# Gathering the last edge slots of a group's first block for 32 or 64 nodes instead of 128

## The chip, the cores and the metric

The kernel runs on one core of a Trainium2 chip. The metric is the device time of one launch in microseconds (us); the number given for a kernel is the median of several runs.

A core has a matrix engine (PE, with its weight load PEld), a vector engine (DVE), a scalar engine (ACT), a general engine (POOL) and a queue engine (SP). On-chip memory has 128 partitions, so a tile holds up to 128 nodes, one per partition. Plain transfers are issued from SP. Transfers whose rows are picked by a list of indices (gathers and scatters, "indirect DMAs") are issued from POOL.

## The reference

One layer of a graph network over 6,250 nodes with 256 features and 206,250 directed edges (100,000 random pairs in both directions, and a loop for each node). What matters here is the attention over edges:

```python
xn = _layernorm(x, axis=-1)
q, k, v = xn @ Wq.T + bq, xn @ Wk.T + bk, xn @ Wv.T + bv      # 8 heads of 32
sim = (q[dst] * k[src]).sum(head) / sqrt(32)                   # one number per edge and head
attn = softmax of sim over the edges with the same dst
agg[n] = sum over edges with dst == n of attn * v[src]
x = x + agg @ Wo.T + bo + linear_attention(xn)
x = x + mixture_of_experts(_layernorm(x))                      # 8 experts, each node goes to one
```

The edges come sorted by `dst`, so each node's sources lie next to each other, and a node's degree is the number of its edges: 33 on average.

## The kernel before

**Tables.** A first stage (about 138 us) computes keys and values of all nodes, block by block of 128, and writes them to a table in device memory, `kv_tab`, with 512 floats (2 KB) per node.

**Groups and blocks.** The 49 blocks of nodes form three groups of 20, 17 and 12 blocks (`GROUPS`). In each group the nodes are sorted by falling degree (`rank_group`), and the sorted nodes are cut into blocks of 128 again. So the first block of a group (block 0, 20 and 37) holds the nodes with the most edges, the highest degree in partition 0. A block has a fixed number of slots (`SLOTS`, from `planned_slots`); slot `j` holds the `j`-th edge of each of its 128 nodes. A first block has 62 slots, since it has to hold the node of the highest degree; the second blocks have 43, 43 and 41. All blocks together have 1,715 slots. A node with fewer edges than slots has rows of other edges in the rest; they are masked by a large negative number (`late`, L1358).

**Units and chunks.** A block's slots are cut into units of at most 44 slots (a first block has two units of 31), and a unit into chunks of four or five (`W = 5`). A chunk is one buffer `kvg` of a ring of 11 (`kvp`, `RING`). For each slot one indirect DMA on POOL (L627) brings the 128 rows of `kv_tab` that the slot's indices name, 256 KB. In the main loop (from L1355 on) the DVE multiplies the keys of a chunk by the queries (L1373) and adds them up per head (L1374). After a unit's last chunk comes the softmax, and the values of this unit are weighted on the DVE (L1325) and added by the PE (matmul with the identity, L1329, into `pa`) while the keys of the next unit are worked on. Only then is the buffer free again. POOL's instructions stand in one order: `gather_to(at + 1 + LEAD)` lets the gathers run ahead of the keys by `LEAD = 2` chunks in that order, and in time POOL goes as far ahead as free buffers of the ring let it.

**Work beside.** `background` puts pieces of other work between the chunks, paced by the number of slots: in group 0's attention the queries, the sorting of the other groups (`other_ranks`) and the linear attention; in group 1's and 2's attention the output projection, routing and experts of the group before (`behind`). This work starts with the second unit of a group's first block at the latest. After the last group's attention its own experts follow with nothing beside them.

**Guard.** `other_ranks` compares each node's degree with its block's slots (L687, `over`). If any node has more, a flag is set and a general path runs after the fast one.

Of the kernel before, what the change touches and what calls it, by code (L numbers as in the profile page):

```python
# [42 lines left out]
def planned_slots(n_nodes, n_edges, groups):  # L43

    lam = max(1.0, n_edges / n_nodes - 1.0)
    pm = [math.exp(-lam)]
    for k in range(1, 1000):  # L50
        pm.append(pm[-1] * lam / k)
    more = [sum(pm[k:]) for k in range(len(pm))]
    out, b0 = [], 0
    for g in groups:
        m = min(n_nodes - b0 * P, g * P)
        for j in range(g):
            k = 1
# [5 lines left out]
            out.append(k)  # L63
        b0 += g
    return out

# [2 lines left out]
def gps_layer(  # L69
# [50 lines left out]
    C = max(1, math.ceil(1.25 * N / NX))  # L120
    MI = MH * MD
    HP = MI // P
    SLOTS = planned_slots(N, E, GROUPS)
    SMAX = max(SLOTS)
    scale = 1.0 / math.sqrt(GD)

# [31 lines left out]
    with tc.manual_schedule():  # L158
# [207 lines left out]
        with ExitStack() as actx:  # L366
# [210 lines left out]
            for b in order:  # L577
                S = SLOTS[b]
                n_p = -(-S // PART)
                cut = [S * i // n_p for i in range(n_p + 1)]  # L580
                for i in range(n_p):
                    n = cut[i + 1] - cut[i]
                    n_ch = -(-n // W)
                    cuts = [cut[i] + n * k // n_ch for k in range(n_ch + 1)]
                    units.append((b, i, n_p, cut[i], cut[i + 1], list(zip(cuts, cuts[1:]))))
            chunk_list = [(u, k) for u in range(len(units)) for k in range(len(units[u][5]))]
            UMAX = max(u[4] - u[3] for u in units)
            idx_of, qs_of, kv_of = {}, {}, {}
# [24 lines left out]
            def gather_to(k):  # L613

                nonlocal pool_at
                while pool_at < min(k, len(chunk_list)):
                    u, c = chunk_list[pool_at]
                    b, part, _, _, _, chunks = units[u]
                    i = order.index(b)
                    if c == 0 and part == 0 and i > 0:  # L620
                        sources(i + 1)
                        queries(i + 1)
                    j0, j1 = chunks[c]
                    kv = kvp.tile([P, W, 2 * D], F32, name="kvg")
                    kv_of[u, c] = kv
                    for j in range(j0, j1):
                        nc.gpsimd.indirect_dma_start(  # L627
                            out=kv[:, j - j0, :], out_offset=None, in_=kv_tab[:, :],
                            in_offset=bass.IndirectOffsetOnAxis(ap=idx_of[b][:, j : j + 1], axis=0),
                        )  # L630
                    pool_at += 1

# [48 lines left out]
        def other_ranks():  # L681
            t = rank_consts(mp1)
            for g in range(1, NG):
                yield from rank_group(g, t, mp1, mp2)
            bs = list(range(NB))
            for b in bs:
                nc.vector.tensor_scalar(over[:, b : b + 1], deg_r[:, b : b + 1], float(SLOTS[b]), None, op0=ALU.is_gt)  # L687
                if b % 8 == 7:
                    yield 1.5
            nc.vector.tensor_reduce(bad[:, 1:2], over, AX.X, ALU.max)  # L690
# [624 lines left out]

        def weigh(v, c):

            j0, j1 = v["chunks"][c]
            m = j1 - j0
            kv = kv_of.pop((v["u"], c))  # L1320
            if c == 0:
                v["pa"] = qps.tile([P, D], F32, name="pa")
            s0, s1 = v["s0"], v["s1"]
            vals = kv[:, :m, D:].rearrange("p j (h d) -> p j h d", d=GD)
            nc.vector.tensor_tensor(  # L1325
                vals, vals, v["pr"][:, j0 - s0 : j1 - s0, :, None].to_broadcast([P, m, GH, GD]), ALU.mult
            )
            for j in range(m):
                nc.tensor.matmul(  # L1329
                    v["pa"], ident, kv[:, j, D:], start=(j0 + j == s0), stop=(j0 + j == s1 - 1),  # L1330
                )

        def complete(v):
# [21 lines left out]
        for u, (b, part, n_p, s0, s1, chunks) in enumerate(units):  # L1355
# [4 lines left out]
            )  # L1360
            sim = cp2.tile([P, UMAX, GH], F32, name="sim")[:, :n, :]
            n_v = len(v["chunks"]) if v else 0
            for c in range(max(len(chunks), n_v)):
                work = pace[group_of[b]] * (chunks[c][1] - chunks[c][0] if c < len(chunks) else W)
                background(work / 2)
# [2 lines left out]
                background(work / 2)  # L1368
                if c < len(chunks):
                    gather_to(at + 1 + LEAD)  # L1370
                    j0, j1 = chunks[c]
                    keys = kv_of[u, c][:, : j1 - j0, :D]
                    nc.vector.tensor_tensor(keys, keys, qc[:, None, :].to_broadcast([P, j1 - j0, D]), ALU.mult)  # L1373
# [588 lines left out]
```

## Time and profile before

| | us |
|---|---|
| median of 3 runs | 3531.13 (3529.72 to 3541.31) |
| profiled execution | 3071.36 |
| its span, first to last instruction | 3069.6 |

The profiled execution is 460 us shorter than the median of the runs. The profile doesn't show why.

Busy time of each engine in stretches of the profiled execution (us from the start of its span):

| stretch | what runs | length | PE | DVE | POOL |
|---|---|---|---|---|---|
| 0 to 138 | keys, values, first sort | 138 | 118.36 | 88.29 | 52.38 |
| 138 to 480 | group 0's attention, its first blocks | 342 | 196.98 | 251.35 | 224.15 |
| 480 to 1200 | rest of group 0, start of group 1 | 720 | 535.27 | 598.97 | 547.03 |
| 1200 to 1365 | group 1, its first blocks | 165 | 119.04 | 145.64 | 104.55 |
| 1365 to 2100 | rest of group 1, start of group 2 | 735 | 540.54 | 476.65 | 550.58 |
| 2100 to 2250 | group 2, its first blocks | 150 | 99.22 | 119.00 | 77.20 |
| 2250 to 2740 | rest of group 2 | 490 | 393.37 | 290.35 | 340.49 |
| 2740 to 3069 | last group's experts and output | 329 | 214.93 | 56.47 | 27.46 |

An engine that is busy for a large part of a stretch need not be its limit; the waits say which one is. A POOL instruction for an indirect DMA counts as busy only while it runs, and each is followed by a gap of 0.30 us, so that a POOL with nothing to wait for shows about three quarters.

### The profile page before, as it was taken

What the parts mean: (1) busy time and instruction counts of PE and PEld (TensorE: products, weight loads), DVE (VectorE), ACT (ScalarE), POOL (GpSimd) and SP (SyncE); (2) the same over time, 40 slices, a digit from 0 to 9 for tenths busy, and PEclk for the clock granted to TensorE, in tenths of its full rate; (3) what the DMA queues carried; (4) which work ended last, traced back from release to release, by engine and by line L of the source; (5) the groups of instructions that cost most, each with busy time, mean ns of one, the idle gap of its engine ahead of it and who ended that gap; (6) DMA issues with size and microseconds to landing.
All of it is one profiled execution on the core that took longest, in us unless ns stands there. A gap on an engine that the chain in (4) does not pass through costs nothing. (4 is left out here: it accounts for less than half of the span.)

```text
span 3069.6 us, 29584 instructions
## 1 busy us (share of the span) xinstructions
PE 2217.7 (72%) x9090; PEld 1731.0 (56%) x9090; DVE 2026.7 (66%) x2728; ACT 638.1 (21%) x1800; POOL 1923.8 (63%) x2114
## 2 busy tenths in 40 slices
PE   8756548788788655764989988445629999856494
PEld 4335335555555444643777877334528888735494
DVE  5658868898888767884767766566845666664000
ACT  4300003343434101210111111101202122112242
POOL 4366767777777777567777777776466767650101
PEclk9867779999898778876999999678859999978797
DMA  7675876777777668767888887777668988753783
GB/s 256 212 248 171 268 260 201 213 211 213 208 206 221 199 197 262 250 195 234 307 285 307 294 301 248 223 204 248 198 188 279 321 300 311 241 179 111 279 327 111
DMA packets 294378, 728.05 MB, mean 237 GB/s; under 512 B 47142, under 2 KB 156292, under 8 KB 280900
## 3 DMA queue, kind: packets, MB, share of 16 engines
q0 software_dynamic: 149744, 477.83, 50.7%
q1 hardware_dynamic: 144468, 248.24, 23.2%
q8 instruction: 75, 1.23, 0.2%
q14 instruction: 91, 0.75, 0.1%
HBM read 652.25 MB, written 73.64 MB: 236 GB/s over the span
## 5 line engine op out<-in xcount | busy, mean ns | idle before, releaser
L627 POOL DMA_INDIRECT kvg<-kv_tab,idx x1715 | 1628.3, 949 | 650.7 <-issue 463.2
L1329 PE MATMUL pa<-kvg,ident 128*128 128x256 f32 x3430 | 1008.4, 451 | 583.3 <-DVE kvg L1325 420.6
L1329 PEld LDWEIGHTS pa<-kvg,ident 128*128 128x128 f32 x3430 | 756.9, 227 | 817.1 <-DVE kvg L1325 501.4
L1373 DVE TENSOR_TENSOR kvg<-kvg,qc 128x1280 f32<-128x1280 f32 (+1 forms) x366 | 512.4, 1400 | 389.3 <-DMA kvg<-kv_tab,idx 326.7
L1374 DVE TENSOR_REDUCE sim<-kvg 128x40 f32<-128x1280 f32 (+1 forms) x366 | 513.2, 1402 | 12.6
L1325 DVE TENSOR_TENSOR kvg<-kvg,pr 128x1280 f32<-128x1280 f32 (+1 forms) x366 | 509.3, 1393 | 0.0
L1204 PE MATMUL bank<-wt,hTe 128*128 128x256 f32 x1056 | 247.7, 382 | 0.0
L1187 PE MATMUL bank<-xTe,wt 128*128 128x256 f32 x1056 | 242.6, 381 | 2.3 <-ACT xTe L1177 2.3
L1187 PEld LDWEIGHTS bank<-xTe,wt 128*128 128x128 f32 x1056 | 201.6, 191 | 30.5 <-ACT xTe L1177 3.0
L1204 PEld LDWEIGHTS bank<-wt,hTe 128*128 128x128 f32 x1056 | 201.7, 193 | 27.5
L1268 DVE TENSOR_TENSOR res<-bank,row_b 128x256 f32<-128x256 f32 x49 | 20.6, 421 | 280.8 <-ACT bank L1264 272.6
L751 PE MATMUL bank<-wm,xTm 128*128 128x512 f32 x392 | 178.0, 597 | 0.0
L1247 POOL DMA_INDIRECT row_a<-ybuf,row_from x49 | 46.5, 948 | 197.6 <-DMA ybuf<-res 173.0
L1193 ACT ACTIVATE hTe<-bank,wt 128x256 f32<-128x256 f32 x264 | 110.8, 471 | 266.0 <-PE bank L1187 266.0
L1210 ACT COPY res<-bank 128x256 f32<-128x256 f32 x85 | 31.7, 372 | 424.5 <-PE bank L1208 236.1
L751 PEld LDWEIGHTS bank<-wm,xTm 128*128 128x128 f32 x392 | 72.1, 194 | 71.6 <-issue 71.3
L1301 ACT COPY qc<-qs 128x256 f32<-128x256 f32 x49 | 18.8, 384 | 442.9 <-DVE kvg L1373 412.0
L843 POOL DMA_INDIRECT xbuf<-row_a,row_to x49 | 48.0, 980 | 96.6 <-DVE cmp L1088 67.5
L537 PE MATMUL pkv<-wn,xT 128*128 128x512 f32 (+1 forms) x276 | 106.0, 540 | 3.5 <-DVE kv L552 3.5
L843 POOL DMA_INDIRECT agg_tab<-ag,node_ri x49 | 48.5, 990 | 91.2 <-DVE ag L1347 68.4
L1173 PE MATMUL bank<-ident,in 128*128 128x128 f32 x170 | 28.7, 283 | 100.4 <-DMA in<-xbuf 100.4
L780 ACT ACTIVATE ck<-bank,rk 128x64 f32<-128x64 f32 x392 | 86.2, 341 | 28.9 <-DVE rk L777 28.4
(258 smaller groups left out, 2208.4 us busy)
## 6 DMA issues: line engine op xcount, KB each, us to landing
wt<-in_w_rows_dram SPq DMA_DIRECT2D x33, 1152.0 KB, 8.2
wt<-in_w_rows_dram SPq DMA_DIRECT2D x33, 1028.0 KB, 7.9
kvg<-kv_tab,idx POOLq DMA_INDIRECT x1715, 4.0
kvg<-in_w_rows_dram SPq DMA_DIRECT2D x19, 1152.0 KB, 6.1
kvg<-in_w_rows_dram SPq DMA_DIRECT2D x19, 1028.0 KB, 7.7
kv_tab<-kv SPq DMA_DIRECT2D x49, 256.0 KB, 2.7
in<-xbuf SPq DMA_DIRECT2D x85, 128.0 KB, 8.7
ybuf<-res SPq DMA_DIRECT2D x85, 128.0 KB, 3.4
```

Source lines behind the costliest of these rows:

```text
L537: nc.tensor.matmul(done[i], xTs[b // GX][:, b % GX, c, :], wn[:, c, w], start=(c == 0), stop=(c == DC - 1))
L627: nc.gpsimd.indirect_dma_start(out=kv[:, j - j0, :], out_offset=None, in_=kv_tab[:, :], in_offset=bass.IndirectOffsetOnAxis(ap=idx_of[b][: ...
L751: nc.tensor.matmul(pm, xT_of[b][:, c, :], wmf[:, c, s * MI : (s + 1) * MI], start=(c == 0), stop=(c == DC - 1),)
L780: nc.scalar.activation(cks[b][:, h, :], pms[b][0][:, h * MD : (h + 1) * MD], AF.Copy, scale=rk[:, h : h + 1])
L843: s = nc.gpsimd.indirect_dma_start(**kw)
L1187: nc.tensor.matmul(ph[:, k, :], w[:, c, f * P : (f + 1) * P], T[t]["xT"][:, c, :size], start=(k == 0 and c == 0), stop=(k == 1 and c == DC ...
L1193: nc.scalar.activation(T[t]["hT"][:, f, :size], ph[:, k, :], AF.Relu, bias=w1_t[:, V1 + f : V1 + f + 1])
L1204: nc.tensor.matmul(py, T[t]["hT"][:, f, k * P : (k + 1) * P], w[:, f, :], start=(f == 0), stop=False)
L1325: nc.vector.tensor_tensor(vals, vals, v["pr"][:, j0 - s0 : j1 - s0, :, None].to_broadcast([P, m, GH, GD]), ALU.mult)
L1329: nc.tensor.matmul(v["pa"], ident, kv[:, j, D:], start=(j0 + j == s0), stop=(j0 + j == s1 - 1),)
L1373: nc.vector.tensor_tensor(keys, keys, qc[:, None, :].to_broadcast([P, j1 - j0, D]), ALU.mult)
L1374: nc.vector.tensor_reduce(sim[:, j0 - s0 : j1 - s0, :], keys.rearrange("p j (h d) -> p j h d", d=GD), AX.X, ALU.add)
```

## The change

`planned_slots` now returns, for each block, a list with a number of nodes for each slot. In a group's first block it works out from a Poisson distribution of degrees how many of the group's nodes are expected to use slot `s`, adds 2.5 standard deviations and 1, and takes the smallest of 32, 64 and 128 that is not below it. All slots of other blocks keep 128. For this input, block 0 and 20 get 45 slots of 128, 2 of 64 and 15 of 32; block 37 gets 44, 2 and 16. Since the nodes are sorted, the first partitions are those with the most edges.

Chunks are now cut so that all slots of one have the same number of nodes. The second units of the first blocks had seven chunks of 4, 4, 5, 4, 4, 5, 5 slots; in block 0 and 20 they have seven of 4, 5, 5 (128 nodes), 2 (64) and 5, 5, 5 (32), in block 37 eight of 4, 4, 5, 2, 4, 4, 4, 4. The number of slots, 1,715, stays. In a chunk of `n` nodes the gather, both multiplications, the reduction and the matmul use partitions 0 to `n` only. The entries of `sim` of these slots are set to 0 first (one memset of the DVE for each of the three units), so that the other partitions have a value there, which the mask makes negligible. The guard compares in a first block partitions 0 to 31, 32 to 63 and 64 to 127 with their own number of slots (62, 47 and 45; in block 37 62, 46 and 44).

```diff
+            nodes = [P] * k
+            for s in range(k if j == 0 else 0):
+                p = more[s]
+                need = m * p + 2.5 * math.sqrt(max(0.0, m * p * (1 - p))) + 1
+                nodes[s] = next(n for n in (32, 64, P) if need <= n or n == P)
+            out.append(nodes)
...
-                    n_ch = -(-n // W)
-                    cuts = [cut[i] + n * k // n_ch for k in range(n_ch + 1)]
-                    units.append((b, i, n_p, cut[i], cut[i + 1], list(zip(cuts, cuts[1:]))))
+                    chunks = []
+                    for nodes in (P, 64, 32):
+                        js = [j for j in range(cut[i], cut[i + 1]) if NODES[b][j] == nodes]
+                        n_ch = -(-len(js) // W)
+                        cuts = [js[0] + len(js) * k // n_ch for k in range(n_ch + 1)] if js else []
+                        chunks += [(j0, j1, nodes) for j0, j1 in zip(cuts, cuts[1:])]
+                    units.append((b, i, n_p, cut[i], cut[i + 1], chunks))
...
                         nc.gpsimd.indirect_dma_start(
-                            out=kv[:, j - j0, :], out_offset=None, in_=kv_tab[:, :],
-                            in_offset=bass.IndirectOffsetOnAxis(ap=idx_of[b][:, j : j + 1], axis=0),
+                            out=kv[:n, j - j0, :], out_offset=None, in_=kv_tab[:, :],
+                            in_offset=bass.IndirectOffsetOnAxis(ap=idx_of[b][:n, j : j + 1], axis=0),
                         )
...
-                nc.vector.tensor_scalar(over[:, b : b + 1], deg_r[:, b : b + 1], float(SLOTS[b]), None, op0=ALU.is_gt)
+                for p0, n in ((0, P),) if min(NODES[b]) == P else ((0, 32), (32, 32), (64, 64)):
+                    q = slice(p0, p0 + n)
+                    most = sum(m > p0 for m in NODES[b])
+                    nc.vector.tensor_scalar(
+                        over[q, b : b + 1], deg_r[q, b : b + 1], float(most), None, op0=ALU.is_gt
+                    )
...
-            vals = kv[:, :m, D:].rearrange("p j (h d) -> p j h d", d=GD)
+            vals = kv[:n, :m, D:].rearrange("p j (h d) -> p j h d", d=GD)
             nc.vector.tensor_tensor(
-                vals, vals, v["pr"][:, j0 - s0 : j1 - s0, :, None].to_broadcast([P, m, GH, GD]), ALU.mult
+                vals, vals, v["pr"][:n, j0 - s0 : j1 - s0, :, None].to_broadcast([n, m, GH, GD]), ALU.mult
             )
             for j in range(m):
                 nc.tensor.matmul(
-                    v["pa"], ident, kv[:, j, D:], start=(j0 + j == s0), stop=(j0 + j == s1 - 1),
+                    v["pa"], ident[:n, :], kv[:n, j, D:], start=(j0 + j == s0), stop=(j0 + j == s1 - 1),
                 )
...
+            few = [j0 for j0, _, m in chunks if m < P]
+            if few:
+                nc.vector.memset(sim[:, few[0] - s0 :, :], 0.0)
...
-                    keys = kv_of[u, c][:, : j1 - j0, :D]
-                    nc.vector.tensor_tensor(keys, keys, qc[:, None, :].to_broadcast([P, j1 - j0, D]), ALU.mult)
+                    keys = kv_of[u, c][:m, : j1 - j0, :D]
+                    nc.vector.tensor_tensor(
+                        keys, keys, qc[:m, None, :].to_broadcast([m, j1 - j0, D]), ALU.mult
+                    )
                     nc.vector.tensor_reduce(
-                        sim[:, j0 - s0 : j1 - s0, :], keys.rearrange("p j (h d) -> p j h d", d=GD), AX.X, ALU.add
+                        sim[:m, j0 - s0 : j1 - s0, :], keys.rearrange("p j (h d) -> p j h d", d=GD), AX.X, ALU.add
                     )
```

More of the change, by code (lines that the diff above doesn't have):

```diff
@@ L62, in planned_slots @@
                 k += 1
-            out.append(k)
+            nodes = [P] * k
[4 more added lines that the diff above has]
+            out.append(nodes)
         b0 += g
@@ L122, in gps_layer @@
     HP = MI // P
-    SLOTS = planned_slots(N, E, GROUPS)
+    NODES = planned_slots(N, E, GROUPS)
+    SLOTS = [len(n) for n in NODES]
     SMAX = max(SLOTS)
@@ L622, in gather_to @@
                         queries(i + 1)
-                    j0, j1 = chunks[c]
+                    j0, j1, n = chunks[c]
                     kv = kvp.tile([P, W, 2 * D], F32, name="kvg")
@@ L1316, in weigh @@
         def weigh(v, c):
-            j0, j1 = v["chunks"][c]
+            j0, j1, n = v["chunks"][c]
             m = j1 - j0
@@ L1370, in gps_layer @@
                     gather_to(at + 1 + LEAD)
-                    j0, j1 = chunks[c]
-                    keys = kv_of[u, c][:, : j1 - j0, :D]
-                    nc.vector.tensor_tensor(keys, keys, qc[:, None, :].to_broadcast([P, j1 - j0, D]), ALU.mult)
+                    j0, j1, m = chunks[c]
+                    keys = kv_of[u, c][:m, : j1 - j0, :D]
+                    nc.vector.tensor_tensor(
+                        keys, keys, qc[:m, None, :].to_broadcast([m, j1 - j0, D]), ALU.mult
+                    )
                     nc.vector.tensor_reduce(
-                        sim[:, j0 - s0 : j1 - s0, :], keys.rearrange("p j (h d) -> p j h d", d=GD), AX.X, ALU.add
+                        sim[:m, j0 - s0 : j1 - s0, :], keys.rearrange("p j (h d) -> p j h d", d=GD), AX.X, ALU.add
                     )
```

## The prediction

> **What bounds the kernel now.** I read the engines' shares of the span first, then the groups of instructions, then POOL's own order of time, and last who waits for whom just behind the slots that the change touches.
>
> ```profile
> PE 2217.7 (72%) x9090; PEld 1731.0 (56%) x9090; DVE 2026.7 (66%) x2728; ACT 638.1 (21%) x1800; POOL 1923.8 (63%) x2114
> L627 POOL DMA_INDIRECT kvg<-kv_tab,idx x1715 | 1628.3, 949 | 650.7 <-issue 463.2
> L1373 DVE TENSOR_TENSOR kvg<-kvg,qc 128x1280 f32<-128x1280 f32 (+1 forms) x366 | 512.4, 1400 | 389.3 <-DMA kvg<-kv_tab,idx 326.7
> ```
>
> No engine looks full, but two rows name the bound of the attention: the gathers' POOL instructions are followed by 463 us of "issue", gaps in which POOL waits for nothing visible, and the DVE waits 327 us for gathered data. POOL's order of time shows the gap:
>
> ```profile
> 600.20 0.94 POOL L627 DMA_INDIRECT kvg<-kv_tab,idx  x1 [0.30 <-issue]
> 601.45 0.95 POOL L627 DMA_INDIRECT kvg<-kv_tab,idx  x1 [0.30 <-issue]
> 602.70 0.95 POOL L627 DMA_INDIRECT kvg<-kv_tab,idx  x1 [0.30 <-PE pa L1329]
> ```
>
> A gather starts every 1.25 us: 0.95 and a fixed 0.30. From 475 to 1250 us POOL has no longer gap than that, so there each gather is worth its 1.25 us. The narrow gathers lie elsewhere. Counting L627 in POOL's order, those of block 0 (slots 45 to 61 of a block that starts at the 38th gather) run from 274 to 296 us, block 20's from 1189 to 1210, block 37's from 2088 to 2113. Just behind them (waits of POOL, then of the DVE, from 1212 to 1337 us):
>
> ```profile
> POOL kvg L627 <- PE pa L1329: 13.4, 8, 5.4
> POOL agg_tab L843 <- DVE ag L1347: 6.2, 1, 6.2
> POOL kvg L627 <- PE bank L890: 5.8, 5, 4.5
> ...
> DVE row_b L917 <- PE bank L911: 6.3, 7, 1.4
> DVE rsd L932 <- ACT rsd L926: 3.7, 4, 1.7
> DVE logits L952 <- PE bank L949: 1.4, 1, 1.4
> DVE kvg L1373 <- issue: 1.1, 1, 1.1
> ```
>
> Here POOL waits for free buffers (PE pa is the last reader of one) and for the DVE, and the DVE never waits for gathered data. The same in order of time, POOL's first such waits and the DVE's first wait for data behind each first block:
>
> ```profile
> 336.86 0.94 POOL L627 DMA_INDIRECT kvg<-kv_tab,idx  x1 [2.47 <-PE pa L1329]
> 361.69 1.49 DVE L1373 TENSOR_TENSOR kvg<-kvg,qc 128x1280 f32<-128x1280 f32 x1 [2.61 <-DMA kvg<-kv_tab,idx]
> 1251.54 0.94 POOL L627 DMA_INDIRECT kvg<-kv_tab,idx  x1 [4.54 <-PE bank L890]
> 1337.54 1.49 DVE L1373 TENSOR_TENSOR kvg<-kvg,qc 128x1280 f32<-128x1280 f32 x1 [0.72 <-DMA kvg<-kv_tab,idx]
> 2131.73 0.94 POOL L627 DMA_INDIRECT kvg<-kv_tab,idx  x1 [4.74 <-PE pa L1329]
> 2247.92 1.49 DVE L1373 TENSOR_TENSOR kvg<-kvg,qc 128x1280 f32<-128x1280 f32 x1 [4.55 <-DMA kvg<-kv_tab,idx]
> ```
>
> In all three places POOL is stopped by the full ring before the DVE next lacks data. At the start of a group the work beside is dense on the DVE (57.8 of 63 us busy from 298 to 361, 108.5 of 125 from 1212 to 1337, 106.1 of 132 from 2115 to 2247). So in the profiled execution the DVE is the limit exactly where the change makes POOL faster.
>
> **What the Trainium skill says.** *DMA: Bandwidth & Descriptors*, section "Anatomy of one DMA — SWDGE (gpsimd) path", calls descriptor generation "small, variable" and says "You can emit a lot of descriptors before the incremental cost shows up": a 32-row gather could cost POOL nearly what a 128-row one does. The trace agrees only in that bytes don't matter (0.945 us for an index load of up to 248 B a row, 0.949 for 2 KB); all indirect DMAs here have 128 rows, so it shows no price of a row. *Perfetto Trace Analysis*, section "DMA Instruction — SWDGE (GPSIMD)", says that the instruction's end in the profile is the end of descriptor generation, which fits data that land 4.0 us after the issue. *TensorE: Matmul & The Clock Gate*, section "LDWEIGHTS (loading the stationary operand)": "A 32×128 weight load takes the same time as a 128×128 weight load". *VectorE: DVE Perf Modes*, section "Why `tensor_reduce` can't reduce along partition axis", describes the partitions as independent lanes that stream along the free dimension, so fewer partitions save the DVE nothing. No run shows either with fewer partitions yet.
>
> **The change part by part.**
> - *Narrow gathers.* 46 of 32 rows and 6 of 64. POOL's saving for one lies between 0 (all of it fixed) and the share of missing rows times the whole period. With half of the period per row, the middle of these bounds since no row of the trace narrows them, a 32-row gather saves 0.5 × 0.75 × 1.25 = 0.47 us and a 64-row one 0.31. That is 7.7 us each for block 0 and 20 (15 × 0.47 + 2 × 0.31), 8.1 for block 37, 23.5 in all; at most 47. In the profiled execution all of it goes into POOL's waits for the ring: next late is what is late now, the DVE. Counted on the path: 0.
> - *Fewer bytes.* (46 × 96 + 6 × 64) × 2 KB = 9.8 MB of 728. Where they fall, the DVE doesn't wait for data. 0.
> - *DVE.* The two multiplications and the reduction of a chunk fit 0.16 us + 1.04 ns per element (1.486 us for 1,280, 1.220 for 1,024), by elements per partition, which don't change in sum. One chunk more in block 37: 3 × 0.16 = 0.5. Three memsets of 136 or 144 elements at the 0.19 of the 160-element memset of `ones`: 0.6. Six more comparisons at the 0.143 of `over`: 0.9, at 336 to 351 us. Together 2.0 us on the engine that is full there; what the DVE waits for data soon after hides some of it. 0 to 2.0, taken as 2.0.
> - *PE.* 104 of the 3,430 matmul instructions of L1329 have 32 or 64 rows of weights. Taken at no cost by the skill; what it is if the narrow loads no longer hide is rival C.
> - *Ring and order.* Block 37's second unit has eight chunks, but the second blocks of 41 and 43 slots have nine, so the ring sees nothing new. No instruction of SP, ACT or POOL is added, none moves past another; on the DVE a chunk's work shifts by a piece of work beside at most.
>
> Sum against the profiled execution: 3071.4 + 0 to 2 us.
>
> **From there to the median.** The median, 3531.1, is 459.8 us above the profiled execution, as much as 0.229 us on each of the 2,009 indirect DMAs (1,715 and 6 × 49). The profile can't say whether it lies there. But POOL is what bounds most of the attention, so an extra on another engine would have to exceed POOL's waits first. If it lies on POOL, its period is 1.477 us, and the waits that swallow the saving shrink. That gives the cases.
>
> **A, faster (0.48), the forecast: the extra lies on POOL, and half a gather's period goes by rows.** A 32-row gather then saves 0.554 us, a 64-row one 0.369: 9.05 us each in block 0 and 20, 9.6 in block 37. Slack behind block 0: 2.2 us of POOL waits above 0.30 (298 to 361 us), less 49 DMAs × 0.229 = 11.2: none, so all 9.05 stay. Behind block 20: 11.0 + 5.9 + 4.3 = 21.2 less 84 × 0.229 = 19.2 leaves 2.0, so 7.05 stay. Behind block 37 (2115 to 2247): 46.6 less 72 × 0.229 = 16.5 leaves 30, so nothing stays. 16.1 − 2.0 = 14.1, and 3531.1 − 14.1 = **3517 us**. With all of the period by rows 18.1 + 16.1 − 2.0 = 32.2, so 3499; its own range is 3499 to 3520. Against it: the page on descriptors, and that the place of the 460 us is inferred.
>
> **B, no change (0.35): the ring takes the saving, or a gather's cost is fixed.** As in the profiled execution, for which every line above speaks: 3531 + 0 to 2, about 3532. Against it: the median isn't the profiled execution.
>
> **C, slower (0.17): narrow matmuls break the PE's rhythm.** Ten loads now take 2.02 us beside ten matmuls in 2.43, so they are hidden. If a load for 32 rows isn't hidden, each of the 104 costs its 0.190 us: 19.8, in the chain PE pa to POOL's next gather, which is what POOL waits for behind all three blocks. 3531.1 + 19.8 + 2.0 = 3553. From 0.083 us per instruction it decides (8.6 + 2.0 = 10.6), if no gain stands against it. Against it: the skill's page on the load, and a PE that is at most 0.73 busy in these stretches.
>
> **That the change doesn't do what it says** would be an overflow of the guard: the general path would run as well. In the drawn graph the 33rd and 65th highest degrees are 46 and 44 (group 0), 46 and 45, 45 and 43, against 47 and 45, 47 and 45, 46 and 44 slots. It holds, by no more than an edge or two; I give it nothing.
>
> **Numbers.** What a measurement can tell from no change is about 0.3%, 10.6 us: the three runs lie 11.6 apart. A's chance goes to faster but for a share by rows below 0.4, where it would be within; some of B's unknowns go the other way, so I leave 0.48, 0.35 and 0.17. The range, 3494 to 3545, takes in A with all by rows and 5 us of luck, all of B, and C up to two thirds of its price.
>
> **What would show it.** L627 with a second, shorter duration for 32 rows at 274, 1189 and 2088 us (0.95 again: the cost is fixed, A falls). POOL's waits for PE pa behind the blocks longer by what the gathers save (B in the profiled execution). L1373 with 32 partitions at 1.486 us for five slots. L1329 with 32 rows still about 0.24 us apart (0.43 or more: C). If the profiled execution falls by over 10 us, my reading of the ring is wrong; if the median falls by over 35, the gathers' price is beyond my bounds.

## The result and the profile after

| | median (lowest to highest) | runs |
|---|---|---|
| after | 3545.04 us (3522.79 to 3558.10) | 20 |
| before, beside it | 3532.05 us (3513.34 to 3542.71) | 20 |
| ratio | 1.0035, 95% interval 1.0018 to 1.0051 | |

The change makes the kernel slower by a third of a per cent, 13 us. The forecast was 14 us faster. (The ratios here and below are not the quotients of the two medians and differ from them by up to 0.14%; differences in us are of medians.)

One thing has to be known before any two profiles are compared: the same program takes about 3071 us on some chips and 3502 to 3544 us on others, profiled or not. By its time, the profile of before that the prediction read (span 3069.6 us) is from a chip of the first kind; the timed runs above and the profile after (span 3532.7 us) are from one of the second. The experiments below fell on both kinds, so each ratio is taken against runs of before on its own chip, and profiles of the two kinds are set against each other only to tell the chips apart.

The page of the kernel after, engines first, then the row of the gathers (busy us and mean ns of one; then the engine's idle time before them and what ended most of it):

```profile
PE 2337.3 (66%) x9090; PEld 1784.0 (50%) x9090; DVE 2028.4 (57%) x2740; ACT 630.8 (18%) x1800; POOL 1918.1 (54%) x2114
...
L638 POOL DMA_INDIRECT kvg<-kv_tab,idx x1715 | 1621.4, 945 | 908.1 <-issue 488.3
```

The gathers' mean has gone from 949 to 945 ns, with the 52 narrow ones in it; those of 128 rows alone average 948. So on the chip with 460 us more, POOL's instruction for one gather takes as long as on the other. POOL is only busy for 54% of the time there, and its idle time ahead of gathers has grown from 650.7 to 908.1 us. It waits more, it doesn't work more. Two of the waits that grew, in the profile of before and in the one after (total, times and longest in us):

```profile
POOL agg_tab L843 <- DVE ag L1347: 68.4, 14, 14.3
DVE ag L1347 <- PE pa L1329: 87.3, 17, 22.9
```

```profile
POOL agg_tab L859 <- DVE ag L1363: 264.4, 38, 15.2
DVE ag L1363 <- PE pa L1345: 207.7, 22, 23.3
```

POOL in order of time at the end of the narrow slots of block 0, in the profile after (start, duration, engine and line; in brackets the idle time before):

```profile
333.86 0.86 POOL L638 DMA_INDIRECT kvg<-kv_tab,idx  x1 [0.30 <-issue]
335.02 0.87 POOL L638 DMA_INDIRECT kvg<-kv_tab,idx  x1 [0.30 <-issue]
336.19 0.86 POOL L638 DMA_INDIRECT kvg<-kv_tab,idx  x1 [0.30 <-issue]
...
340.46 0.95 POOL L638 DMA_INDIRECT kvg<-kv_tab,idx  x1 [0.30 <-issue]
```

The first three have 32 rows, the last has 128. On the mean of all 46, a gather of 32 rows takes 0.863 us, and one of 128 has a median of 0.946: three quarters of the rows less save 0.083 us of a period of 1.25, and the gap of 0.30 stays. A 64-row gather takes 0.90 to 0.91. All 52 narrow gathers together save POOL 46 × 0.083 + 6 × 0.04 = about 4 us.

The DVE's groups by shape (mean ns is the second number):

```profile
L1392 DVE TENSOR_TENSOR kvg<-kvg,qc 128x1280 f32<-128x1280 f32 x247 | 366.7, 1485 | 295.8 <-DMA kvg<-kv_tab,idx 196.5 <-issue 68.6 <-PE pa L1345 23.5
L1392 DVE TENSOR_TENSOR kvg<-kvg,qc 32x1280 f32<-32x1280 f32 x6 | 8.8, 1470 | 0.0
```

A quarter of the partitions instead of all of them saves 15 ns of 1485. And the PE's matmuls into `pa` by shape:

```profile
L1345 PE MATMUL pa<-kvg,ident 128*128 128x256 f32 x3326 | 996.2, 455 | 631.3 <-issue 402.7 <-DVE kvg L1341 224.9 <-PE bank L1220 1.7
L1345 PE MATMUL pa<-kvg,ident 32*128 32x256 f32 x92 | 35.0, 545 | 11.7 <-DVE kvg L1341 7.6 <-issue 4.1
L1345 PE MATMUL pa<-kvg,ident 64*128 64x256 f32 x12 | 3.4, 402 | 2.2 <-DVE kvg L1341 1.3 <-DVE mvd L940 1.0
```

On the mean the matmuls of 32 rows take 0.09 us longer than those of 128, and those of 64 don't. A part of that is where they stand: in a kernel with the new chunks and nothing narrow that was run later (the first of the third set), the same 92 matmuls take 481 ns. So the engine with less work, POOL, gains at most 4 us, and something else costs 13 us or more.

### The profile page after: what moved, and what is told of

The parts are those of the page before. It is cut to its first block, busy times and chain, and to the rows that moved or that the text cites. A ratio compares the mean times of both kernels' runs of the same rounds, so it can differ in the third digit from the quotient of the medians.

```text
span 3532.7 us, 29594 instructions
## 1 busy us (share of the span) xinstructions
PE 2337.3 (66%) x9090; PEld 1784.0 (50%) x9090; DVE 2028.4 (57%) x2740; ACT 630.8 (18%) x1800; POOL 1918.1 (54%) x2114
## 5 line engine op out<-in xcount | busy, mean ns | idle before, releaser
L638 POOL DMA_INDIRECT kvg<-kv_tab,idx x1715 | 1621.4, 945 | 908.1 <-issue 488.3
L1345 PE MATMUL pa<-kvg,ident 128*128 128x256 f32 x3430 | 1034.6, 457 | 645.2 <-issue 406.8
L1392 DVE TENSOR_TENSOR kvg<-kvg,qc 128x1280 f32<-128x1280 f32 (+3 forms) x367 | 512.5, 1396 | 341.1 <-DMA kvg<-kv_tab,idx 225.3
L1395 DVE TENSOR_REDUCE sim<-kvg 128x40 f32<-128x1280 f32 (+3 forms) x367 | 513.3, 1399 | 12.6
L1341 DVE TENSOR_TENSOR kvg<-kvg,pr 128x1280 f32<-128x1280 f32 (+3 forms) x367 | 509.4, 1389 | 0.0
L1220 PE MATMUL bank<-wt,hTe 128*128 128x256 f32 x1056 | 266.4, 396 | 42.1 <-issue 40.3
L1363 DVE TENSOR_TENSOR ag<-pa,s 128x256 f32<-128x256 f32 x46 | 19.5, 424 | 336.5 <-PE pa L1345 207.7
L859 POOL DMA_INDIRECT agg_tab<-ag,node_ri x49 | 48.5, 989 | 295.2 <-DVE ag L1363 264.4
L804 PE MATMUL bank<-ck,cv 128*128 128x128 f32 x392 | 72.6, 333 | 143.1 <-ACT ck L796 126.0
L804 PEld LDWEIGHTS bank<-ck,cv 128*128 128x128 f32 x392 | 64.9, 232 | 157.9 <-ACT ck L796 133.3
L784 DVE TENSOR_REDUCE rv<-sq 128x16 f32<-128x1024 f32 x49 | 59.5, 1215 | 142.4 <-ACT sq L776 110.4
L776 ACT ACTIVATE sq<-bank 128x512 f32<-128x512 f32 x98 | 56.9, 596 | 399.1 <-remote 189.3
```

The lines of the kernel that those rows point to most:

```text
L638: nc.gpsimd.indirect_dma_start(out=kv[:n, j - j0, :], out_offset=None, in_=kv_tab[:, :], in_offset=bass.IndirectOffsetOnAxis(ap=idx_of[b][ ...
L776: nc.scalar.activation(sqs[b][:, s * MH : (s + 1) * MH, :].rearrange("p g d -> p (g d)"), pms[b][s], AF.Square)
L784: nc.vector.tensor_reduce(rv, sqs[b], AX.X, ALU.add)
L804: nc.tensor.matmul(dots[:, hp, :], cvs[b][:, h], ckf[:, h], start=(b == 0 and hp == 0), stop=(b == NB - 1 and hp == HP - 1), skip_group_ch ...
L1220: nc.tensor.matmul(py, T[t]["hT"][:, f, k * P : (k + 1) * P], w[:, f, :], start=(f == 0), stop=False)
L1341: nc.vector.tensor_tensor(vals, vals, v["pr"][:n, j0 - s0 : j1 - s0, :, None].to_broadcast([n, m, GH, GD]), ALU.mult)
```

## The experiments

### The cutting, the narrow matmuls and the narrow gathers apart

Edits are shortened to the lines that matter and stand against the change, those of the narrow matmuls and of the reordered and early kernels against the kernel before.

Four kernels on a chip where before takes 3071.32 us (27 runs). The first is the kernel before, unchanged, for a profile beside the others.

> The kernel before once more, unchanged, as a control and for a profile beside which the one of after can be laid. Every theory: ratio 1.000 with an interval of about 0.002 either way. The open point is the profile: if its span is again near 3070 us, profiling shortens this program; if it is near 3530, the first profiled execution of before was not typical, and the durations of waits that the prediction was built on were not those of the timed runs. I expect 3530.

Measured: 3068.69 us, ratio 0.9995 (0.9984 to 1.0006).

The second has the change's chunks alone; gathers, DVE operations and matmuls stay on 128 partitions:

```diff
-                            out=kv[:n, j - j0, :], out_offset=None, in_=kv_tab[:, :],
+                            out=kv[:, j - j0, :], out_offset=None, in_=kv_tab[:, :],
...
-            j0, j1, n = v["chunks"][c]
+            j0, j1, n_pe = v["chunks"][c]
+            n = P
...
                     j0, j1, m = chunks[c]
+                    m = P
```

> Only the new cutting of chunks (4, 5, 5, 2, 5, 5, 5 for 4, 4, 5, 4, 4, 5, 5 slots, eight chunks in block 37), everything on 128 partitions, guard as before. Theory 'order' (the shift of chunks against the work beside makes the 12 us): ratio 1.003 to 1.004. Theory 'narrow matmuls': 1.000. Theory 'narrow gathers' (32-row transfers hurt somewhere): 1.000.

Measured: 3079.28 us, 1.0034 (1.0022 to 1.0045).

The third has the chunks and the 104 narrow matmuls:

```diff
-                    v["pa"], ident, kv[:, j, D:], start=(j0 + j == s0), stop=(j0 + j == s1 - 1),
+                    v["pa"], ident[:n_pe, :], kv[:n_pe, j, D:], start=(j0 + j == s0), stop=(j0 + j == s1 - 1),
```

> The new cutting, and the 104 matmul instructions of the narrow chunks with 32 or 64 rows; gathers and DVE on all 128 partitions. Theory 'narrow matmuls' (the page of after shows 0.545 us for one of 32 rows, 0.455 for one of 128): 1.003 or more, as much as the whole change. Theory 'order': the same as the run with the cutting alone. Theory 'narrow gathers': 1.000.

Measured: 3088.22 us, 1.0061 (1.0042 to 1.0080).

The fourth is the whole change except that the gathers bring 128 rows:

```diff
-                            out=kv[:n, j - j0, :], out_offset=None, in_=kv_tab[:, :],
-                            in_offset=bass.IndirectOffsetOnAxis(ap=idx_of[b][:n, j : j + 1], axis=0),
+                            out=kv[:, j - j0, :], out_offset=None, in_=kv_tab[:, :],
+                            in_offset=bass.IndirectOffsetOnAxis(ap=idx_of[b][:, j : j + 1], axis=0),
```

> The whole change, but the gathers fetch all 128 rows again; DVE, PE, memset and guard as in the change. Theory 'narrow gathers': 1.000, since the gathers alone cost the time. Theories 'order' and 'narrow matmuls': 1.003 to 1.004 as with the whole change, perhaps 4 us (0.001) more, what the shorter gather instructions saved POOL (46 x 0.08 + 6 x 0.04 us).

Measured: 3083.22 us, 1.0047 (1.0030 to 1.0064).

The loss is there without a narrow gather, and 8 us of it without anything narrow at all. The narrow matmuls add 8.9 us in the third kernel, 3.9 in the fourth (six runs each). The change as it is was not run on a chip of this kind.

I took the start of each block's scatter into `agg_tab` as a mark, 49 of them, and compared the marks of each kernel with those of the kernel before. The distance grows at two places: between the scatters that enclose the work on block 20's second unit (by 3.6 us in the second kernel, 7.0 in the third, 7.4 in the fourth) and on block 37's (by 3.8, 9.4 and 6.1). Elsewhere it stays within about 2.5 us once the first four blocks are through. Between the two profiles of the kernel before, this one and the one that the prediction read, no such step is longer than 0.9 us there, so these two are more than the scatter of one execution. Behind block 0, where the work beside is the ranks and queries, the three kernels differ in sign, and the two profiles of before differ by 4.3 us.

What the DVE waited for between the two scatters around block 37's units, first in the kernel before (2082.8 to 2216.8 us), then with the change's chunks alone (2082.7 to 2220.4 us); total, times and longest in us:

```profile
DVE row_b L917 <- PE bank L911: 16.7, 6, 11.6
DVE logits L952 <- PE bank L949: 7.7, 4, 2.5
DVE rsd L932 <- ACT rsd L926: 5.8, 5, 2.3
```

```profile
DVE row_b L933 <- PE bank L927: 23.4, 11, 13.1
DVE logits L968 <- PE bank L965: 7.6, 4, 2.9
DVE rsd L948 <- ACT rsd L942: 3.4, 4, 1.7
```

These are steps of the output stage of the group before (`output_stage`, run by `background`): the PE multiplies by the output weights (into `bank`), and one piece later the DVE reads the product (`row_b`). The DVE takes its instructions in order, so while it waits there the next chunk waits too. With the new chunks it waits for `row_b` at 11 places instead of 6, while its busy time is the same (97.18 us before, 97.49 with the chunks). The DVE in order of time around the two-slot chunk of block 37 shows one such place:

```profile
2115.80 1.21 DVE L1342 TENSOR_TENSOR kvg<-kvg,pr 128x1024 f32<-128x1024 f32 x1
2116.92 0.16 DVE L948 RECIPROCAL rsd<-rsd 128x1 f32<-128x1 f32 x1
2117.12 0.21 DVE L949 TENSOR_SCALAR rsd<-mvd,rsd 128x1 f32<-128x1 f32 x1
2117.25 0.68 DVE L1394 TENSOR_TENSOR kvg<-kvg,qc 128x512 f32<-128x512 f32 x1
2117.96 0.69 DVE L1397 TENSOR_REDUCE sim<-kvg 128x16 f32<-128x512 f32 x1
2121.53 0.17 DVE L968 TENSOR_TENSOR logits<-bank,gb 128x8 f32<-128x8 f32 x1 [2.89 <-PE bank L965]
2123.85 0.48 DVE L933 SCALAR_TENSOR_TENSOR row_b<-bank,rstd,row_a 128x256 f32<-128x256 f32 x1 [2.15 <-PE bank L927]
```

As I read it, a chunk of four has 2.4 us of keys on the DVE (1.22 twice) behind which a PE step can finish; the chunk of two has 1.4. The two stretches, with all of the DVE's waits for `row_b`, `rsd` and these `logits` in them, whatever ended the wait (us):

| | block 20: length, waits | block 37: length, waits |
|---|---|---|
| before | 111.6, 14.7 | 134.0, 32.7 |
| new chunks | 115.1, 19.3 | 137.7, 35.6 |
| and narrow matmuls | 118.5, 22.4 | 143.4, 41.5 |
| all narrow but the gathers | 119.1, 23.1 | 140.1, 38.7 |

Without these waits every kernel takes 95.8 to 96.9 us in the first stretch and 101.3 to 102.1 in the second: the waits are the whole of what the stretches grow by. Over the whole profiled execution they come to 85.5 us in the kernel before, and to 92.8, 102.3 and 99.1 us in the three others: 7.3, 16.8 and 13.6 more, beside 8.0, 16.9 and 11.9 us more in the medians. On the faster chips, then, the loss has the size of these waits.

### The change with the chunks cut as before

The next four ran on a chip where before takes 3501.99 us (59 runs). The first is the change as it is.

> The whole change, beside the kernel before on the chip of these runs. All theories: it keeps the loss of the blind test, ratio 1.0035 to 1.006. The 32-row gathers come out at 0.86 us and the 64-row ones at 0.90 against 0.945, about 4 us of GpSimd in all; if these lay on the path here the ratio would be below that of the cutting alone (1.0034), if they don't it is above it by what the narrow matmuls cost (0.001 to 0.003).

Measured: 3515.39 us, 1.0029 (1.0003 to 1.0055): the loss is there again.

The second has everything narrow, but in the old chunks; a chunk is as narrow as its widest slot allows, 32 partitions for 14 slots of each first block and 64 for four more of block 37:

```diff
-                    for nodes in (P, 64, 32):
-                        js = [j for j in range(cut[i], cut[i + 1]) if NODES[b][j] == nodes]
...
+                    n_ch = -(-n // W)
+                    cuts = [cut[i] + n * k // n_ch for k in range(n_ch + 1)]
+                    chunks = [(j0, j1, NODES[b][j0]) for j0, j1 in zip(cuts, cuts[1:])]
```

> Narrow gathers, narrow DVE operations and narrow matmuls, but the chunks cut as before (4, 4, 5, 4, 4, 5, 5), each as narrow as its widest slot allows: 14 slots a block stay narrow. Order theory (the new sizes of the chunks put pieces of the work beside against too little DVE work): the steps of 3.6 to 3.8 us at block 20's and block 37's units go, only the narrow matmuls' cost is left, ratio 1.000 to 1.002. Narrow-operation theory (what is narrow costs, however cut): ratio stays at 1.0035 or more. Forecast's theory (narrow gathers gain once the rest is undone): below 0.998.

Measured: 3509.30 us, 1.0007 (0.9990 to 1.0024).

The third has the old chunks and only the matmuls narrow, the fourth is the second with 64 partitions wherever that has 32.

> Chunks cut as before, gathers and DVE operations on all 128 partitions, only the matmuls of 42 slots (84 instructions) with 32 rows. Matmul theory (32-row matmuls lower the granted clock to about 0.5 while they run): 84 x 0.1 to 0.2 us, of which a part is on the path, ratio 1.001 to 1.003 and the clock in the windows of these slots at 0.5 to 0.6. Order theory alone: ratio 0.999 to 1.001. Rival C as predicted (loads not hidden, 0.19 us each): 16 us, ratio 1.005.

> As the second kernel of this set, but 64 partitions wherever that one uses 32. If the matmul's cost comes from few rows, 64-row matmuls take 0.40 us as the twelve of the change do, the granted clock stays at 0.8, and the ratio is 0.999 to 1.001; if any narrow matmul costs, it is as that one, 1.001 to 1.002.

Measured: 3503.11 us, 0.9991 (0.9973 to 1.0009), and 3506.70 us, 1.0003 (0.9985 to 1.0021). With the old chunks no loss is clear of the noise, narrow or not. But the median of the second is 7.3 us above before's, its interval allows 8.4 (0.0024), and it overlaps that of the change: this set points to the chunks, it doesn't show them alone. The matmul's price was missed here: the interval of the third allows 3 us at most. And the mean of a few narrow matmuls says little by itself: the fourth's 92 of 64 rows average 504 ns, the same 92 on 128 rows 485 in a kernel with the old chunks on another chip (the second of the next set).

### The chunks or the pieces between them

The new sizes act in two ways: they are the DVE's and PE's steps, and each gives `background` a credit in proportion, which decides where its pieces fall. On a chip where before takes 3543.98 us (40 runs) I parted the two, with all operations on 128 partitions. First the new chunks with the credit of the old ones, then the mirror:

```diff
-                work = pace[group_of[b]] * (chunks[c][1] - chunks[c][0] if c < len(chunks) else W)
+                work = pace[group_of[b]] * (steps_of(n, chunks)[c] if c < len(chunks) else W)
```

> The change's cutting alone (all operations on 128 partitions), but the credit for the work beside is given out chunk by chunk as before (4, 4, 5, 4, 4, 5, 5; nothing for the eighth chunk of block 37). If the loss comes from where the pieces of the work beside land, the steps at block 20's and 37's units go: ratio 0.999 to 1.001. If it comes from the sizes of the chunks themselves (a short one covers less of a wait, another chunk costs an overhead), the cutting's loss stays: 1.0025 to 1.004.

> The mirror: chunks cut as before, the credit for the work beside given out in the change's steps (4, 5, 5, 2, 5, 5, 5; for block 37 4, 4, 5, 2, 4, 4, 8). Placement of the pieces: 1.002 to 1.004. Sizes of the chunks: 0.999 to 1.001. If the first two kernels both come out near 1.002, both have a part.

Measured: 3555.40 us, 1.0039 (1.0023 to 1.0055), and 3543.24 us, 0.9993 (0.9970 to 1.0015). With the old credit the loss stays, with the new credit alone it isn't there: it is the chunks themselves. My first idea, that a changed credit puts the pieces elsewhere, fell.

The third kernel is a dose of narrow matmuls; it leaves out the sums of 96 of each 128 nodes:

```diff
-                    v["pa"], ident, kv[:, j, D:], start=(j0 + j == s0), stop=(j0 + j == s1 - 1),
+                    v["pa"], ident[:32, :], kv[:32, j, D:], start=(j0 + j == s0), stop=(j0 + j == s1 - 1),
```

> A dose: the kernel before with the matmuls of all 1,715 slots on the first 32 rows, so the output leaves out the gathered sums of 96 of each 128 nodes; everything else as before. If 32-row matmuls lower the granted clock, as short windows of the earlier runs suggest, the mean clock falls well below that of before over the whole attention and the ratio is 1.01 or more; if that was chance, the clock and the time stay, ratio 0.998 to 1.002. Rival C (0.19 us for each of 3,430) would give over 1.05 where POOL waits for the PE.

Measured: 3651.53 us, 1.0297 (1.0256 to 1.0338). Two lines from the page of the kernel with the old chunks and full matmuls (the second of this set), and the same two from the dose. PEclk is the granted clock of the PE in 40 slices, in tenths; L764 is a matmul of the linear attention that both kernels have in the same form:

```profile
PEclk9867777988778777896889888866876999987697
...
L764 PE MATMUL bank<-wm,xTm 128*128 128x512 f32 x392 | 197.4, 651 | 0.0
```

```profile
PEclk9855557777777655765798887755766999875797
...
L764 PE MATMUL bank<-wm,xTm 128*128 128x512 f32 x392 | 226.7, 732 | 0.0
```

With 32-row matmuls between them, unchanged full matmuls take 732 instead of 651 ns, and the mean clock falls from 0.815 to 0.727. Ahead of the attention (0 to 138 us) and behind it (from 3256 and 3350 us on), where neither kernel has these matmuls, the two clocks are the same, 0.94 and 0.83. So narrow matmuls lower the clock for all that the PE does in that stretch; they don't lengthen only themselves. The dose costs 107.6 us for 3,430 matmuls, 0.031 us each.

The fourth puts the two 64-row slots back to 128, so that the units are cut more evenly, without a chunk of two and without an eighth:

```diff
-                nodes[s] = next(n for n in (32, 64, P) if need <= n or n == P)
+                nodes[s] = next(n for n in (32, P) if need <= n or n == P)
```

> The change with only two widths, 32 and 128: the two slots of 64 go back to 128, so the units are cut 4, 4, 4, 4, 5, 5, 5 and, in block 37, 5, 5, 5, 4, 4, 4, 4: seven chunks, none of two slots; 46 slots stay narrow on all engines. Order theory, if it is the short chunk and the eighth chunk that cost: 0.998 to 1.001. If any other cutting than before's costs: 1.002 to 1.004.

Measured: 3562.24 us, 1.0053 (1.0028 to 1.0078), more than either outcome that I had named. The next two sections come back to it.

### A dose of sizes, and the waits taken away

On a chip where before takes 3504.45 us (67 runs): first the kernel before with the same sizes in another order in every unit, fours first and then fives; second the even cutting alone, with nothing narrow.

```diff
-                    cuts = [cut[i] + n * k // n_ch for k in range(n_ch + 1)]
+                    size, more = divmod(n, n_ch)
+                    cuts = [cut[i] + k * size + max(0, k - (n_ch - more)) for k in range(n_ch + 1)]
```

> The kernel before with the chunks of every unit sorted, all fours first and then the fives, in place of fours and fives spread evenly; the same number of chunks and nothing narrow. If a less even order of sizes costs by itself, all first blocks and every stretch with the output stage beside pay: 1.003 or more. If only the first blocks' own place matters, about 1.001 to 1.003. If sizes were chance, 0.999 to 1.001.

> The cutting with widths of 32 and 128 alone (4, 4, 4, 4, 5, 5, 5 and, in block 37, 5, 5, 5, 4, 4, 4, 4), all operations on 128 partitions. Sizes: 1.002 to 1.004, and the rest of the 1.0053 measured with narrow operations is the matmuls'. If the cutting is free, 0.999 to 1.001, and the narrow matmuls make all of the 1.0053.

Measured: 3521.65 us, 1.0048 (1.0031 to 1.0065), and 3501.80 us, 0.9996 (0.9980 to 1.0012). Nothing but the order of fours and fives costs 17 us when all units have it, and nothing that can be measured when only the first blocks' second units have it. So the order of sizes does matter in this kernel; a unit without a chunk of two came off free.

Third and fourth, the kernel before and the change with the output stage's second PE step issued one piece earlier, so that it has a piece more to finish before the DVE reads it:

```diff
                 if j < ng:
                     s1(j)
+                    s2(j)
...
-                if j < ng:
-                    s2(j)
```

> The kernel before with the output stage's second PE step (the product with the output weights) issued in the same piece as the first, one piece ahead of the DVE step that reads it. If the DVE's waits for it (57.5 us in the kernel before on the faster chip) are on the path, ratio 0.985 to 0.997 and the row_b waits fall to under half; if something else is late next (the PE waits for ACT's copy of the turned rows, then the gathered data), 0.998 to 1.002.

> The whole change with the same early step. If the change loses its time on those waits, it now stands at most 0.0015 above the kernel with the early step alone (the narrow matmuls' share); if the loss comes another way, it stands 0.003 or more above it, as the change does above before.

Measured: 3508.57 us, 1.0014 (0.9998 to 1.0031), and 3509.02 us, 1.0006 (0.9982 to 1.0030). The change's cost on top of the early step is gone (the medians are 0.5 us apart), which is what the theory of these waits asks for; but the interval of the second still reaches to 1.003, and the change without the early step was not run on this chip, so this supports it and doesn't settle it. And the early step itself gains nothing, because other waits come in its place. The DVE's waits in the profile of the kernel before with the early step (`remote` is something that the trace doesn't name):

```profile
DVE logits L952 <- PE bank L949: 41.2, 22, 3.5
DVE row_b L917 <- PE bank L911: 25.0, 4, 9.3
DVE logits L952 <- remote: 22.7, 4, 7.3
```

`row_b` is waited for at 4 places now, but the step after it in the same chain, `logits`, at 22. (In the run of the same kind of chip with old chunks and new credit, the two lines of L911's and L949's counterparts read 46.3 us at 23 places and 10.6 at 6.)

### The even cutting again

The last two fell on a chip where before takes 3070.51 us (35 runs): the even cutting with narrow matmuls only, and with all operations narrow.

> The even cutting with narrow matmuls (92 instructions with 32 rows), gathers and DVE operations on 128 partitions. Dose price of a 32-row matmul (0.031 us of time each): 0.999 to 1.002. If narrow matmuls cost more where the output stage lies beside them: 1.004 or more.

> The even cutting with all operations narrow, the same program as h1_even_cuts. If it again stands 0.004 or more above before, and the matmuls alone don't, narrow gathers or DVE operations cost here; if it comes out at 0.998 to 1.002, the 1.0053 of the first time does not hold from chip to chip and the even cutting saves the change's loss.

Measured: 3077.44 us, 1.0020 (1.0011 to 1.0028), and 3074.47 us, 1.0012 (1.0000 to 1.0024). The 1.0053 does not hold from chip to chip: the same program costs between nothing and 0.24% here. Why it cost more there stays open. Narrow matmuls cost 6.9 us, 0.075 us for each of the 92, if the cutting is free on this chip too, which was measured only on the other kind. The DVE's waits for `row_b`, `rsd` and `logits` over the whole execution are 10.3 and 15.3 us above the 85.5 of before, while the medians are 6.9 and 4.0 above: as a sum they are a rough guide, and only the two stretches can be matched closely.

In which way they cost can be read from the PE in order of time. Chunks behind block 20, in the kernel before on this kind of chip (1250 to 1277 us), and in the one with new chunks and narrow matmuls (1256 to 1286 us):

```profile
1250.68 4.01 PE L1329 MATMUL pa<-kvg,ident 128*128 128x256 f32 x10 [2.60 <-DVE kvg L1325]
...
1264.19 2.43 PE L1329 MATMUL pa<-kvg,ident 128*128 128x256 f32 x10 [1.69 <-DVE kvg L1325]
...
1276.12 2.43 PE L1329 MATMUL pa<-kvg,ident 128*128 128x256 f32 x10 [1.37 <-DVE kvg L1325]
```

```profile
1269.62 3.60 PE L1346 MATMUL pa<-kvg,ident 32*128 32x256 f32 x10 [2.21 <-DVE kvg L1342]
1278.47 2.42 PE L1346 MATMUL pa<-kvg,ident 32*128 32x256 f32 x10
1285.00 2.42 PE L1346 MATMUL pa<-kvg,ident 32*128 32x256 f32 x10 [0.91 <-DVE kvg L1342]
```

Each line is one chunk of five slots, ten matmuls. At full clock (1.00 in the windows of the shorter lines) ten take 2.43 us, whether they have 128 rows or 32: the narrow weight loads are hidden. A chunk takes 3.6 to 4.6 us where the granted clock is low (0.50 to 0.65), with either width. What the narrow ones change is how often it is low: around block 37's units the mean clock is 0.88 in the kernel with the new chunks and full matmuls, first, and 0.82 in this one (stretch, length, busy us and instructions of PE, PEld, DVE, ACT and POOL, then the mean clock, the DMA share and GB/s):

```profile
2082.70:2220.40 137.70, 91.95 (x430) 75.57 (x430) 97.49 (x186) 32.69 (x77) 74.04 (x79) 0.88 0.74 229
```

```profile
2090.90:2234.30 143.40, 100.01 (x430) 79.86 (x430) 97.44 (x186) 32.69 (x77) 73.95 (x79) 0.82 0.73 220
```

The timed runs say the same. On the chip of the first set their mean clock is 0.855 for the kernel before and for the new chunks alone, 0.849 with the narrow matmuls and 0.850 in the fourth kernel; on this chip it is 0.854 before, 0.851 in both.

## Why the prediction was wrong, point by point

- **The step that failed is "Ring and order".** It counted the new chunks at nothing, since "the ring sees nothing new" and a chunk's work shifts "by a piece of work beside at most". The first half held. The second half names the cost and doesn't price it: at the start of groups 1 and 2 the DVE has next to no idle time but its waits for the PE and ACT in the output stage, and other sizes of chunks leave these waits less covered. The cutting alone cost 8.0 us (3079.28 − 3071.32) on one kind of chip and 11.4 (3555.40 − 3543.98) on the other, beside 13.0 for the whole change in the table of the result. The prediction's own view of the DVE's waits just behind block 20 showed those for `row_b`, `rsd` and `logits`, 11.4 us in 125, and it quoted them only to say that the DVE did not wait for data. A second term at nothing, the narrow matmuls, comes below, and the gain that was to stand against both was priced too high.
- **Narrow gathers.** The bound below, most of the cost fixed, was nearly right. By the Trainium skill's *DMA: Bandwidth & Descriptors*, section "Anatomy of one DMA — SWDGE (gpsimd) path", descriptor generation costs little more for more descriptors; the runs agree: 0.863 us for 32 rows and 0.946 for 128. Of a gather's period about 9% goes by rows (0.083 / (0.75 × 1.25)), where the prediction took half: 4 us for 23.5 on POOL. Whether these 4 us reach the time can't be told: with the even cutting the kernel with narrow gathers and DVE operations came out 3.0 us below the one without (3074.47 for 3077.44), and the intervals overlap.
- **Where the median's extra 460 us lies.** The forecast put them on the gathers, 0.229 us each. The trace after, on a chip that has them, shows 948 ns for a gather of 128 rows. What grew is waiting: POOL's scatters wait 264.4 us for the DVE's `ag` where the profile of before has 68.4, and `ag` waits 207.7 us for the PE where it had 87.3 (and 121.5 for something that the trace doesn't name), at a mean clock of 0.81 for 0.855. What makes the chips differ stays open. The prediction had argued that an extra elsewhere "would have to exceed POOL's waits first"; POOL waits for others there. Without this inference case A has no gain left, and the profiled execution's own sum, 0 to 2 us, would have been the forecast.
- **DVE.** 2.0 us were forecast; its busy time rose from 2026.7 to 2028.4, by 1.7. Right, and what the Trainium skill says of independent lanes (*VectorE: DVE Perf Modes*, section "Why `tensor_reduce` can't reduce along partition axis") agrees with 1.470 us for 32 partitions and 1.485 for 128.
- **PE and rival C.** The Trainium skill's page *TensorE: Matmul & The Clock Gate*, section "LDWEIGHTS (loading the stationary operand)", says that a load of 32 rows takes as long as one of 128. The runs agree: ten narrow loads and matmuls go in 2.42 us, ten of 128 rows in 2.43. But the prediction took from this that narrow matmuls cost nothing, and that doesn't follow. Rival C's mechanism, loads that are no longer hidden, is refuted by that; its price of 0.190 us a matmul is too high. Narrow matmuls do cost, by a lower clock: 0.031 us each in the dose, 0.075 in the last set, 0.086 in the first (8.9 us for 104), so 3 to 9 us for 104. In the run with the old chunks nothing of it could be measured. The side, slower, was C's; the larger part of the way was not.
- **Ring (case B).** It described POOL well: what the gathers save goes into waits. It missed what the new chunks do to the DVE.

The parts need not add up: 8 to 11 us of cutting, 3 to 9 us of clock, less at most some 4 us of gathers, against 13.0 and 13.4 us measured for the whole change in two runs on slower chips. What is shown, on a chip of each kind, is that the chunks' sizes alone cost 8 to 11 us. That they act through the DVE's waits for the output stage is shown by traces on the faster chips, and supported by the early step on a slower one; there single executions scatter over 40 us. How cutting and narrow operations share the loss on the slower chips isn't settled: the even cutting was free on one of them, and with narrow operations it cost 18.3 us on another. None of the versions is faster than the kernel before by more than its interval.

## What to carry to other kernels

Where an engine's only idle time is its waits for another with which it takes turns, the sizes of the steps are a schedule: price a change of them by the waits that are already there in that stretch, not at nothing. Count what a smaller operation saves from its smallest measured unit, here a gather's 0.946 us, of which a quarter of the rows still costs 0.863. And before a difference between a profile and a median is put on one kind of instruction, ask whether they are from the same chip.

## What the runs showed of the hardware

- POOL's instruction for a gather of 2 KB rows takes 0.863 us for 32 rows, 0.906 for 64 and 0.946 for 128, each with a gap of 0.30 before the next.
- Matmuls with 32 rows of weights lower the clock that is granted to the PE, also for full matmuls around them: 0.727 on the mean against 0.815, and 732 ns against 651 for the same matmul.
- One program, unchanged, takes 3071 us on some chips and 3502 to 3544 on others. POOL's gather instructions of 128 rows take the same time on both, 949 and 948 ns; the waits between engines are longer on the second kind. How long a gather's data take to land there isn't in the traces.
